# A fused attention and mixture-of-experts layer: the first unit spread by chunks, the last tokens combined by pieces, one small background piece a half step, tails by one queue, VectorE copies in the last unit

## The chip, the cores and the metric

The kernel runs on one core of a Trainium2 chip. The time is the device time of one execution in microseconds (us); "the median" is over several executions. A separate execution was recorded by the hardware profiler, and all rows of the profile are of that one. Engines are written PE (TensorE; PEld are its weight loads), DVE (VectorE), ACT (ScalarE), POOL (GpSimd) and SP (SyncE, which here only issues DMAs). "SPq" and "ACTq" are DMA issues from the queue of SP or ACT.

## What is computed

The input `x` is 8 sequences of 1024 tokens of 256 numbers, all float32. Two stages follow each other, each with a residual:

```
x = x + layernorm(attention(layernorm(x)))     # 16 heads of 16, causal softmax, output matrix Wo
x = x + layernorm(moe(layernorm(x)))           # router over 8 experts, softmax, the best 2 of 8
moe:  gate, up = x @ gate_up[e] + bias         # 256 -> 2 x 512
      act = (clip(up) + 1) * gate * sigmoid(1.702 * gate)
      out = sum over the two experts of weight * (act @ down[e] + bias)
```

## The kernel before, in words

**Attention.** The work is cut into 32 units (`u`): a sequence `b` of 8 and a group `g` of 4 heads. For a unit, q and k of the 4 heads lie in the tiles `qP` and `kP`, each head in 16 rows of its own band of 32 partitions; `spread` (L614) brings them there by eight DMAs from the projected tiles `unq` and `unk`. A unit has nine steps (`STEPS`, L634 to L647), each with two pairs of heads, so 18 half steps. A unit passes through twice: first the maxima of its scores are found (`maxima_tiles`, scores `sa`, L693), then, one unit later, the scores are made again transposed (`values_tiles`, scores `sb`, L788), ACT takes the exponential (L796), and the weighted sums with v are accumulated in `av` (L825). So in the main loop (L1144) a half step holds the `sa` scores of one pair of unit u and the `sb` scores of one pair of unit u-1, the sums of an earlier step, and then pieces of background work. Step 0 of a unit reads only the first 512 columns of `kP` and `qP`.

**Background pieces.** Everything else is written as generators that yield the cost of their next piece on PE, DVE, ACT and POOL: preparing the next sequence (`prep`: layernorm, transposes `xps`), its projections (`project`, `values`), the normalising of the sums (`normalize`, transposes `avt`), the output matrix (`finish`: transposes `aps`, product `yps`) and the routing (`route`: transposes `x2ps`, logits `lpsT`, counts `cps`). Three lists (urgent, due, back) hold the jobs. `earn` (L1079) adds credit for each engine every half step, `affordable` (L1083) finds the first piece that credit allows, `spend` (L1091) emits one, and `pump` (L1102) emits pieces until none is affordable. Pieces of 1.75 us on PE are emitted in place of the sums of the first pair (`whole`, L1203), and in the half steps that hold both kinds of scores `pump` is called with `most=1.0` (L1220), which admits pieces of up to 1.0 us on PE. The tiles in PSUM for `sb` and for all pieces come from one pool of three banks (`ps_b`). Within the attention stage PE, DVE, ACT and SP run in the order of the source (L1131).

**The start.** `begin` (L456) loads and transposes the weights, normalises the 1024 tokens of the first sequence in two chunks of 512, and projects q and k of group 0 chunk by chunk (`project_chunk`, L595; the results are copied by ACT, L602). Half of the normalising steps are ACT's (L488), half DVE's (L486). When both chunks are done, `spread(0)` (L1137) issues q's DMAs from SP and k's from ACT (L622). Then `others` (L525) issues its loads from SP (router weights `rwr`, biases), and its pieces follow: the transposes of Wv and Wo, of `rwr` (L544) and of the biases (L548).

**The experts.** Every token is scattered by POOL (indirect DMAs, L1044) into the regions of its two experts in `xs_dram`. When the last tokens are routed, `fill_tails` (L252) writes 256 rows of zeros behind each expert's last row, eight DMAs, odd experts from ACT's queue and even ones from SP's, each with an address that the issuing engine reads from a table. 71 tiles of 256 rows then pass through gate, up and down (`quarter`, `lower_half`); the rest of the background is pumped in the first ten tiles, and what is left is forced out (`finish_all`, L1460). The loads of tile i+2 are issued from SP at tile i.

**The end.** `both(t)` (L1351) combines 512 tokens: it loads `x1` and the two experts' rows (`yy`, 1 MB, L1358), weighs and adds them in four blocks of 128 tokens (ACT L1372, DVE L1377), takes mean and variance of each block, then one reciprocal root for all four (POOL, L1389), and normalises, adds and writes 512 KB (L1408). The last call stands after the last tile.

Of the kernel before, what the change touches and what calls it, by code (L numbers as in the profile page):

```python
# [17 lines left out]
P = 128  # L18
EPS = 1e-5
# [39 lines left out]
def attn_moe_kernel(  # L59
# [192 lines left out]
    def fill_tails():  # L252

        tail = small.tile([P, E], F32, tag="tail", name="tail")
        nc.vector.tensor_tensor(tail, counts[:, NT, :], region[:, 0, :], ALU.add)
        itail = small.tile([P, E], I32, tag="itail", name="itail")
        nc.vector.tensor_copy(itail, tail)
        for e in range(E):
            queue, engine = (
                (nc.scalar, mybir.EngineType.Activation) if e % 2  # L260
                else (nc.sync, mybir.EngineType.SP)
            )
            at = loaded(itail[0:1, e : e + 1], E * R, engine)
            apart(queue.dma_start(out=slot_rows(at), in_=zeros), "xs")

# [146 lines left out]
    with ExitStack() as attn:  # L412
# [43 lines left out]
        def begin():  # L456
# [54 lines left out]
            for t in range(NC):  # L511
                if t:
                    for kt in range(KT):
                        turn_x(0, t, xn, kt)
                for name in ("q", "k"):
                    project_chunk(0, 0, name, t)
            for mx in mxs:
                in_order(nc.gpsimd.memset(mx, NEG))
            for vp in vps:
# [91 lines left out]
                    yield piece(pe=1.75, act=0.6, after=0 if c else 1)  # L611
                    project_chunk(b, g2, name, c)

        def spread(u):  # L614

            b, g = divmod(u, NG)
            row = qPs[u % NU].rearrange("(h r) (a n s) -> h r a n s", r=HS, n=TN, s=D)
            for a in range(S // (TN * D) if u >= NU else 0):
                nc.sync.dma_start(out=row[:, DH, a], in_=zeros[:HG, :, :D])
            for name, dsts in (("q", qPs), ("k", kPs)):  # L620

                queue = nc.scalar if u == 0 and name == "k" else nc.sync  # L622
                for hh in range(HG):
                    queue.dma_start(
                        out=dsts[u % NU][ds(hh * HS, DH), :],
                        in_=uns[b, g // 2, name][ds((g % 2 * HG + hh) * DH, DH), :],
                    )


# [237 lines left out]
        def finish(b, c):  # L867
# [223 lines left out]
        def spend(least=0.0, most=9.0):  # L1091


            found = affordable(least, most)
            if found:
                kind, job = found
                for i, cost in enumerate(job.cost):
                    credit[i] -= cost
                emit(kind, job)
            return found is not None  # L1100
# [30 lines left out]
        with tc.manual_schedule(  # L1131
# [12 lines left out]
            for u in range(B * NG + 1):  # L1144
# [12 lines left out]
                for k in range(K):  # L1157
# [15 lines left out]
                    for pair in range(2):  # L1173
# [22 lines left out]
                        if first and second:  # L1196
# [3 lines left out]
                            if pair:  # L1200
                                halves = (0, 1) if whole else (1,)
                            else:
                                whole = spend(least=1.5) and bool(late) and (  # L1203
                                    len({t[0] for t in STEPS[late[0][1]][2]}) == 1
                                )
                                halves = () if whole else (0,)
# [141 lines left out]
        yield  # L1348


    def both(t):  # L1351

        x1 = ap2.tile([P, NTB, D], F32, tag="y", name=f"x1_{t}")
        nc.sync.dma_start(out=x1, in_=x1_dram[t])
        yy = x_buffer(f"yy_{t}")[:, : NTB * TOPK * D].rearrange(
            "p (n r d) -> p n r d", n=NTB, r=TOPK
        )
        load = nc.sync.dma_start(  # L1358
            out=yy,
            in_=yt_dram[ds(t * TB * TOPK, TB * TOPK), :].rearrange(  # L1360
                "(p n r) d -> p n r d", p=P, n=NTB
            ),
        )
        ahead_of(load, "yt")
# [3 lines left out]
        mv = small.tile([P, NTB, 2], F32, tag="mv", name="mv")  # L1368

        for n in range(NTB + 1):  # L1370
            if n < NTB:
# [12 lines left out]
        ve = small.tile([P, NTB], F32, tag="ve", name="ve")  # L1384
        nc.vector.tensor_scalar(
            ve, mv[:, :, 1:2].rearrange("p n c -> p (n c)"), EPS, None, ALU.add
        )
        rstd = small.tile([P, NTB], F32, tag="rstd", name="rstd")
        in_order(nc.gpsimd.tensor_tensor(rstd, ve, nhalf, ALU.pow))  # L1389
        yield  # L1390
        yield

        shift = small.tile([P, NTB], F32, tag="shift", name="shift")
        nc.vector.scalar_tensor_tensor(
            shift, mv[:, :, 0:1].rearrange("p n c -> p (n c)"), -1.0, rstd, ALU.mult, ALU.mult
        )
        yield
        o = ap2.tile([P, NTB, D], F32, tag="aT", name=f"o_{t}")
        for n in range(NTB + 1):
            if n < NTB:  # L1400
                nc.scalar.activation(
                    o[:, n, :], acc[:, n, :], AF.Identity,
                    bias=shift[:, n : n + 1], scale=rstd[:, n : n + 1],
                )
            if n:
                nc.vector.tensor_tensor(o[:, n - 1, :], o[:, n - 1, :], x1[:, n - 1, :], ALU.add)
            yield
        nc.sync.dma_start(out=out_t[t], in_=o)  # L1408

    def tiles_for(r):  # L1410

# [5 lines left out]
    with tc.manual_schedule(engines={engines.PE, engines.DVE, engines.Activation}):  # L1417
# [95 lines left out]
```

## Time and profile before

| what | us |
|---|---|
| median of 3 runs | 2243.09 (2241.66 to 2244.4) |
| profiled execution, its own time | 2249.26 |
| its span | 2247.5 |
| start, first scores to the end of unit 0's own part | 31 to 70 |
| units with both kinds of scores | 70 to 1385 |
| the last unit's sums | 1385 to 1420 |
| experts, with background until 1510 | 1420 to 2222 |
| after the last product | 2222 to 2247.5 |
| PE busy over the span | 2178.3 (97%) |
| DVE, ACT, POOL busy | 1641.6, 1092.2, 1063.8 |

How to read the rows: a line of the timeline has the start in us from the span's beginning, the duration, the engine, the line of the source, the operation, the tile written and the tiles read, the shapes, the number of instructions merged into the row, and in brackets the idle time of the engine just before it with what ended it. The ends of matmuls are modelled, so that a matmul that waits may look like a long one. A float32 matmul appears as two instructions.

### The profile page before, as it was taken

To read this page: it belongs to the slowest core of one execution; us is meant where nothing else is said; L and a number is where in the kernel's file an instruction comes from. 1 tells how busy PE (TensorE), PEld (TensorE's weight loads), DVE (VectorE), ACT (ScalarE), POOL (GpSimd) and SP (SyncE) were. 2 spreads that over 40 slices of the span, in tenths; PEclk is the share of its full clock that TensorE was granted. 3 is DMA by queue.
4 is the path that set the end of the run, shared out by engine and by line. 5 is a ranking of instruction groups with operands and counts; after the bars stand their busy time and mean duration, and the time that the engine had idled before them with its cause. 6 is when DMAs were issued, how large, how long until landed. Compare 5 with 4: busy or idle time off the path is not lost.

```text
span 2247.5 us, 45169 instructions
## 1 busy us (share of the span) xinstructions
PE 2178.3 (97%) x16801; PEld 1362.9 (61%) x16801; DVE 1641.6 (73%) x3766; ACT 1092.2 (49%) x2181; POOL 1063.8 (47%) x1228
## 2 busy tenths in 40 slices
PE   7999999999999999999999999989999999999995
PEld 3444444445444445445445444678888888888884
DVE  4766777767767877777777787576568888888775
ACT  3466665665666666666656666522122222322222
POOL 3321463573563472573472463364444444454543
PEclk9899999999999999999999999999999999999998
DMA  3101102101111111211111111676567877877773
GB/s 81 35 6 40 21 21 59 36 24 41 48 30 38 51 30 30 59 30 29 51 39 21 49 49 40 214 218 207 200 227 262 267 264 267 270 245 270 246 250 104
DMA packets 140659, 251.17 MB, mean 112 GB/s; under 512 B 17472, under 2 KB 103384, under 8 KB 138392
## 3 DMA queue, kind: packets, MB, share of 16 engines
q1 hardware_dynamic: 125720, 210.90, 30.3%
q0 software_dynamic: 12960, 35.54, 4.2%
q8 instruction: 133, 2.18, 0.4%
q10 hardware_dynamic: 1760, 1.84, 0.3%
q14 instruction: 86, 0.70, 0.1%
HBM read 175.74 MB, written 55.76 MB: 103 GB/s over the span
## 4 chain that ended last, share of the span: by engine, by line
PE 82%; DVE 10%; POOL 4%; issue 3%; ACT 1%; DMA 1%; POOLq 0%; SPq 0%; ACTq 0%; DVEq 0%
PE sa L693 20%; PE gu L1300 17%; PE av L825 12%; PE dn L1331 8%; PE sb L788 7%; PE vps L584 3%; PE yps L884 3%; PE pjk L598 3%; PE pjq L598 3%; PE avt L856 1%; DVE acc L1377 1%; PE xtps L1280 1%; DVE act L1321 1%; POOL pT L805 1%; DVE gate L1309 1%
## 5 line engine op out<-in xcount | busy, mean ns | idle before, releaser
L796 ACT ACTIVATE pT<-sb 128x512 f32<-128x512 f32 x1152 | 625.5, 595 | 411.7 <-PE sb L788 388.9
L788 PE MATMUL sb<-qP,kP 32*128 32x512 f32 (+3 forms) x3072 | 717.7, 525 | 3.1 <-ACT pT L796 1.1
L693 PE MATMUL sa<-kP,qP 32*128 32x512 f32 (+3 forms) x3072 | 660.3, 528 | 3.6 <-DVE mx L703 1.7
L1300 PE MATMUL gu<-xsT,wg 128*128 128x256 f32 x2272 | 517.5, 380 | 0.7 <-ACT xsT L1282 0.7
L1300 PEld LDWEIGHTS gu<-xsT,wg 128*128 128x128 f32 x2272 | 432.0, 191 | 59.9 <-ACT xsT L1282 0.9
L805 POOL TENSOR_SCALAR_AFFINE_SELECT pT<-pT 128x512 f32<-128x512 f32 x256 | 159.3, 638 | 578.0 <-ACT pT L796 568.4
L709 DVE TENSOR_REDUCE mx<-sa 128x2 f32<-128x1024 f32 x256 | 311.6, 1219 | 118.2 <-PE sb L788 114.5
L1311 ACT ACTIVATE sig<-gate 128x256 f32<-128x256 f32 x284 | 118.3, 416 | 564.7 <-DVE gate L1309 561.8
L693 PEld LDWEIGHTS sa<-kP,qP 32*128 32x128 f32 x3072 | 230.3, 185 | 196.5 <-issue 108.3
L825 PE MATMUL av<-pT,vpad 128*32 128x256 f32 (+1 forms) x5120 | 347.2, 368 | 1.2 <-DVE avs L836 0.9
L1316 POOL TENSOR_TENSOR sig<-sig,gate 128x256 f32<-128x256 f32 x284 | 210.7, 744 | 279.4 <-ACT sig L1311 277.5
L788 PEld LDWEIGHTS sb<-qP,kP 32*128 32x128 f32 x3072 | 305.2, 185 | 39.3 <-ACT pT L796 6.9
L825 PEld LDWEIGHTS av<-pT,vpad 128*32 128x32 f32 x5120 | 116.5, 109 | 288.8 <-issue 216.7
L1331 PE MATMUL dn<-wd,act 128*128 128x256 f32 x1136 | 273.3, 381 | 10.8 <-DVE act L1321 10.4
L1309 DVE TENSOR_SCALAR gate<-gu,bs 128x256 f32<-128x256 f32 x284 | 135.7, 478 | 158.2 <-PE gu L1300 143.4
L1331 PEld LDWEIGHTS dn<-wd,act 128*128 128x128 f32 x1136 | 209.2, 190 | 42.6 <-DVE act L1321 17.7
L703 DVE CUSTOM_DVE_ANT_0 sa<-sa,cmask 128x512 f32<-128x512 f32 x256 | 178.2, 697 | 54.7 <-PE sb L788 32.7
L1341 POOL DMA_INDIRECT ytd<-ys,places x142 | 142.3, 1002 | 137.8 <-DVE ys L1337 111.9
L1044 POOL DMA_INDIRECT xsd<-xn,slots x128 | 126.0, 984 | 61.4 <-issue 31.2
L1321 DVE SCALAR_TENSOR_TENSOR act<-up,sig 128x256 f32<-128x256 f32 x284 | 130.4, 459 | 18.3 <-POOL sig L1316 18.3
L718 DVE TENSOR_REDUCE mx<-sa 128x2 f32<-128x512 f32 x128 | 88.0, 688 | 65.4 <-PE sb L788 38.2
L1313 DVE TENSOR_SCALAR up<-gu,bs 128x256 f32<-128x256 f32 x284 | 134.5, 474 | 0.0
(202 smaller groups left out, 2394.8 us busy)
## 6 DMA issues: line engine op xcount, KB each, us to landing
wg<-_L_ffn_gate_up_proj_dram SPq DMA_DIRECT2D x71, 1024.0 KB
wd<-in_L_ffn_down_proj_dram SPq DMA_DIRECT2D x71, 512.0 KB
xs<-xsd SPq DMA_DIRECT2D x67, 258.0 KB
yy<-ytd SPq DMA_DIRECT2D x16, 1024.0 KB
bs<-biasd SPq DMA_DIRECT2D x71, 132.0 KB
x<-in_L_attn_x_dram SPq DMA_DIRECT2D x16, 512.0 KB
qP<-unq SPq DMA_DIRECT2D x128, 64.0 KB
x1d<-y SPq DMA_DIRECT2D x16, 512.0 KB
```

The source lines that it names most:

```text
L693: nc.tensor.matmul(ps[:, hh, ds(at, w)], lhsT=qP[r, ts(i, P)], rhs=kP[r, ds(c * QC, w)], start=True, stop=True,)
L703: nc.vector.tensor_tensor_reduce(out=ps[:, hh, :], in0=ps[:, hh, :], in1=cmask, scale=1.0, scalar=NEG, op0=ALU.add, op1=ALU.max, accum_out ...
L709: nc.vector.tensor_reduce(mx[:, heads, i, 2:3], ps, AX.X, ALU.max)
L788: nc.tensor.matmul(banks[hh][:, ds(at, QC - off)], lhsT=kP[r, ts(j, P)], rhs=qP[r, ds(c * QC + off, QC - off)], start=True, stop=True,)
L796: nc.scalar.activation(pT[:, 2 * pair + hh, :], banks[hh], AF.Exp)
L805: in_order(nc.gpsimd.affine_select(out=d, in_=d, compare_op=ALU.is_ge, fill=0.0, base=0, pattern=[[0, HG], [1, P]], channel_multiplier=-1,))
L825: nc.tensor.matmul(av[ds(hh * HS, HS), ds(off + a - at, z - a)], lhsT=vp[:, j, ds((g * HG + hh) * VS, HS)], rhs=pT[:, hh, a:z],  start=c n ...
L1300: nc.tensor.matmul(ps[:, half, :], lhsT=wg[:, kt, ds(half * FF + f * P, P)], rhs=xT[:, kt, :], start=(kt == 0), stop=(kt == KT - 1),)
L1309: nc.vector.tensor_scalar(gt, ps[:, 0, :], bs[:, f : f + 1], LIMIT, ALU.add, ALU.min)
L1316: in_order(nc.gpsimd.tensor_tensor(sg, sg, gt, ALU.mult))
L1321: nc.vector.scalar_tensor_tensor(act[:, f, :], up, 1.0 - LIMIT, sg, ALU.max, ALU.mult)
L1331: nc.tensor.matmul(ps[:, n, :], lhsT=act[:, f, ts(n, P)], rhs=wd[:, f, :], start=(f == 0), stop=(f == FT - 1),)
```

## The change

It has five parts.

1. *Start.* `spread` takes a range of columns. `begin` calls it after each chunk of 512, so that there are 16 DMAs of half the length in place of 8, all from SP's queue; the call after `begin` is gone. In the second chunk ACT does all four normalising steps.
2. *Pump.* `spend` returns the cost of the piece that it emitted. In the half steps where `most` is 1.0 or less, `pump` admits only pieces below 0.3 us on PE once it has emitted one of 0.3 or more.
3. *Tails.* All eight zero fills are issued from SP's queue, and SP reads the eight addresses.
4. *Last unit.* In `finish` of the first chunk of the last sequence, the copies of `aT` and `y` out of PSUM are DVE's (`tensor_copy`) in place of ACT's.
5. *End.* The last call of `both` loads `yy` by four DMAs, one a block, and takes the reciprocal root, the shift, the normalising and the output write in two halves of two blocks. For other calls the order of the work is as before.

```
-            at = loaded(itail[0:1, e : e + 1], E * R, engine)
-            apart(queue.dma_start(out=slot_rows(at), in_=zeros), "xs")
+            at = loaded(itail[0:1, e : e + 1], E * R)
+            apart(nc.sync.dma_start(out=slot_rows(at), in_=zeros), "xs")
...
-                    if n % 2:
+                    if n % 2 and t == 0:
                         ln_apply(xn[:, n, :], of, mv, rstd, n)
...
                 for name in ("q", "k"):
                     project_chunk(0, 0, name, t)
+                spread(0, ts(t, QC))
...
-        def spread(u):
+        def spread(u, cols=slice(0, S)):
...
-                queue = nc.scalar if u == 0 and name == "k" else nc.sync
                 for hh in range(HG):
-                    queue.dma_start(
-                        out=dsts[u % NU][ds(hh * HS, DH), :],
-                        in_=uns[b, g // 2, name][ds((g % 2 * HG + hh) * DH, DH), :],
+                    nc.sync.dma_start(
+                        out=dsts[u % NU][ds(hh * HS, DH), cols],
+                        in_=uns[b, g // 2, name][ds((g % 2 * HG + hh) * DH, DH), cols],
                     )
...
-                nc.scalar.copy(aT[:, kt, :], ps.rearrange("p n q -> p (n q)"))
+                copy = nc.vector.tensor_copy if last and c == 0 else nc.scalar.copy
+                copy(aT[:, kt, :], ps.rearrange("p n q -> p (n q)"))
...
-                nc.scalar.copy(y[:, ts(n2, 2), :], ps)
+                copy(y[:, ts(n2, 2), :], ps)
...
-            while spend(most=most):
-                pass
+            while True:
+                got = spend(most=most)
+                if not got:
+                    break
+                if got[0] >= 0.3 and most <= 1.0:
+                    most = min(most, 0.29)
...
-            spread(0)
...
-    def both(t):
+    def both(t, final=False):
...
+        if final:
+            for n in range(NTB):
+                nc.sync.dma_start(out=yy[:, n], in_=of[:, n])
+        else:
+            ahead_of(nc.sync.dma_start(out=yy, in_=of), "yt")
...
+        size = NTB // 2 if final else NTB
...
+            if n and n % size == 0:
+                g = slice(n - size, n)
+                nc.vector.tensor_scalar(
+                    ve[:, g], mv[:, g, 1:2].rearrange("p n c -> p (n c)"), EPS, None, ALU.add
+                )
+                in_order(nc.gpsimd.tensor_tensor(rstd[:, g], ve[:, g], nhalf[:, g], ALU.pow))
...
+        for g in (slice(a, a + size) for a in range(0, NTB, size)):
+            nc.vector.scalar_tensor_tensor(
+                shift[:, g], mv[:, g, 0:1].rearrange("p n c -> p (n c)"), -1.0, rstd[:, g],
+                ALU.mult, ALU.mult,
+            )
             yield
+            for n in range(g.start, g.stop + 1):
...
+            nc.sync.dma_start(out=out_t[t][:, g], in_=o[:, g])
...
-            ends.append((0, both(routed[r])))
+            ends.append((0, both(routed[r], r == NT - 1)))
```

More of the change, by code (lines that the diff above doesn't have):

```diff
@@ L258, in fill_tails @@
         for e in range(E):
[L259 to L262, printed above, removed]
-            at = loaded(itail[0:1, e : e + 1], E * R, engine)
-            apart(queue.dma_start(out=slot_rows(at), in_=zeros), "xs")
+            at = loaded(itail[0:1, e : e + 1], E * R)
+            apart(nc.sync.dma_start(out=slot_rows(at), in_=zeros), "xs")
     LATE = 4
@@ L1096, in spend @@
                 kind, job = found
+                found = job.cost
                 for i, cost in enumerate(job.cost):
@@ L1099, in spend @@
                 emit(kind, job)
-            return found is not None
+            return found
         def pump(*us, most=9.0):
@@ L1202, in attn_moe_kernel @@
                             else:
-                                whole = spend(least=1.5) and bool(late) and (
+                                whole = spend(least=1.5) is not None and bool(late) and (
                                     len({t[0] for t in STEPS[late[0][1]][2]}) == 1
@@ L1357, in both @@
         )
[L1358 to L1362, printed above, removed]
-        )
-        ahead_of(load, "yt")
+        of = yt_dram[ds(t * TB * TOPK, TB * TOPK), :].rearrange(
+            "(p n r) d -> p n r d", p=P, n=NTB
+        )
+        if final:
[3 more added lines that the diff above has]
+            ahead_of(nc.sync.dma_start(out=yy, in_=of), "yt")
         yield
@@ L1368, in both @@
         mv = small.tile([P, NTB, 2], F32, tag="mv", name="mv")
+        ve = small.tile([P, NTB], F32, tag="ve", name="ve")
+        rstd = small.tile([P, NTB], F32, tag="rstd", name="rstd")
+        shift = small.tile([P, NTB], F32, tag="shift", name="shift")
+        size = NTB // 2 if final else NTB
         for n in range(NTB + 1):
@@ L1383, in both @@
             yield
[L1384 to L1389, printed above, removed]
+            if n and n % size == 0:
[4 more added lines that the diff above has]
+                in_order(nc.gpsimd.tensor_tensor(rstd[:, g], ve[:, g], nhalf[:, g], ALU.pow))
         yield
         yield
[L1393 to L1397, printed above, removed]
-        o = ap2.tile([P, NTB, D], F32, tag="aT", name=f"o_{t}")
[L1399 to L1406, printed above, removed]
-            yield
-        nc.sync.dma_start(out=out_t[t], in_=o)
+        o = ap2.tile([P, NTB, D], F32, tag="aT", name=f"o_{t}")
+        for g in (slice(a, a + size) for a in range(0, NTB, size)):
[3 more added lines that the diff above has]
+            )
+            yield
+            for n in range(g.start, g.stop + 1):
+                if n < g.stop:
+                    nc.scalar.activation(
+                        o[:, n, :], acc[:, n, :], AF.Identity,
+                        bias=shift[:, n : n + 1], scale=rstd[:, n : n + 1],
+                    )
+                if n > g.start:
+                    nc.vector.tensor_tensor(
+                        o[:, n - 1, :], o[:, n - 1, :], x1[:, n - 1, :], ALU.add
+                    )
+                yield
+            nc.sync.dma_start(out=out_t[t][:, g], in_=o[:, g])
     def tiles_for(r):
```

## The prediction

> **What bounds it.** I read the page first: the PE row, the granted clock and the chain's shares.
>
> ```profile
> PE   7999999999999999999999999989999999999995
> PEclk9899999999999999999999999999999999999998
> PE 82%; DVE 10%; POOL 4%; issue 3%; ACT 1%; DMA 1%; POOLq 0%; SPq 0%; ACTq 0%; DVEq 0%
> ```
>
> TensorE is the bound nearly everywhere, and the change alters none of its arithmetic. So it can win only where TensorE stands still or streams late: in the first slices, inside "busy" half steps, and in the last slice. The timelines of those places come next.
>
> **First unit.** Timeline and windows (us, busy of PE, PEld, DVE, ACT, POOL, then granted clock):
>
> ```profile
> 13.21 8.07 DVE L399 TENSOR_SCALAR xn<-x,mv,rstd 128x256 f32<-128x256 f32 x2
> 21.03 1.65 PE L443 MATMUL xps<-ident,xn 128*128 128x128 f32 x7 [3.56 <-DVE xn L399]
> 27.97 2.52 ACTq L624 DMA_DIRECT2D kP<-unk  x4
> 28.89 0.54 SPq L528 DMA_DIRECT2D rwr<-L_ffn_router_weight_dram  x1
> 30.97 0.44 PE L450 MATMUL wps_o<-ident,wr_o 128*128 128x128 f32 x2 [2.54 <-ACT wvT L451]
> 33.94 2.08 PE L693 MATMUL sa<-kP,qP 32*128 32x512 f32 x4
> 20.00:24.00 4.00, 2.97 (x9) 1.97 (x10) 1.29 (x2) 1.17 (x2) 0.82 (x1) 0.67 0.00 0
> ```
>
> VectorE's two normalising steps take 8.07 us beside GpSimd's memsets (the same form took 0.41 at 9.79), and TensorE waits 3.56. The clock is then 0.67 in that window. Later ACT issues four DMAs before it can empty the weights' transposes: TensorE waits 2.54.
>
> With the change ACT does all four steps. Two took 1.09 from 13.51, so four end near 15.7, before the transposes reach them at 17.2; VectorE's removed steps cost nothing elsewhere. At full speed the second chunk repeats the first: from its first transposes (taken as 1.0, the row of eight at full clock later) to the end of the `unk` copy about 5.5 us, so 22.7 and not 27.9. The 3.56 and about 1.5 of half clock go. But all 16 spreading DMAs (before 8) are now on SP, 0.63 us each (2.53 for four). q of chunk 0 starts at 16.3, k ends at 21.3; chunk 1 runs 21.3 to 26.4. Queued behind are `rwr` (0.54) and `gubr` (0.53), ending near 27.5, and the biases. A 64 KB DMA landed at most 2.2 us after issue (a wait for `kP` ended at 30.80, issue 28.57), so `gubr` is there at 29.7. The first pair of scores needs only chunk 0 and runs near 24; the two small transposes L544 and L548 stand behind it in TensorE's order and wait for those loads; the second pair follows at about 30.0. Before: 33.94. **Gain 3.9.** If each score waited for both chunks (last landing 28.6), the mark would be 31 to 32, a gain of 2; with the loads in time, 7.5. I take 3.9, since the issue rows give it.
>
> The new hole from 25 to 29 costs clock too; before, the rows had half clock after the holes, and I leave that as it is. [...]
>
> **Half steps.** A half step is a pair's maxima scores `sa` and weights' scores `sb`, then weighted sums `av` and background pieces. Two small pieces in one look like this (PE, then ACT):
>
> ```profile
> 495.49 1.09 PE L942 MATMUL x2ps<-ident,xn 128*128 128x128 f32 x8
> 496.51 0.48 PE L693 MATMUL sa<-kP,qP 32*128 32x256 f32 x2
> ...
> 497.33 0.79 PE L788 MATMUL sb<-qP,kP 32*128 32x256 f32 x3
> 498.04 0.64 PE L825 MATMUL av<-pT,vpad 128*32 128x256 f32 x8
> 496.32 1.11 ACT L943 COPY xT<-x2ps 128x512 f32<-128x512 f32 x2
> ```
>
> `av` starts 1.53 after `sa`, where the good steps show 1.07 (495.49 is 0.57 after an `av` at 494.92): 0.46 lost inside "busy" TensorE, since `sb` needs a bank that ACT empties only at 497.4. The planner's costs, followed through the source, put two pieces of 0.3 or more into one half step 28 times. I cut TensorE's rows from 70 to 1385 into 554 half steps and subtracted 1.07 for scores, 0.57 for one `av` (1.0 for several), 0.59, 0.5 or 1.91 for a piece. What is left, in the step itself and in the next: no piece 0.14 and 0.10; one 0.25 and 0.07; two 0.2 and 0.34 (19 cases); two and a transposed maximum 0.21 and 0.53 (9); one and a maximum 0.19 and 0.39. Splitting a double: 0.54 plus an empty step's 0.24 becomes twice 0.32, a gain of 0.14; with a maximum 0.98 becomes 0.90. So 19 x 0.14 + 9 x 0.08 = **3.4**. Upper end: all of the following lateness goes, 19 x 0.34 + 9 x 0.53 = 11.2. Lower: each moved piece brings a lone piece's 0.32 and removes nothing but 0.2, minus 28 x 0.12 = -3.4. I take 3.4, the measured difference of like rows. The pieces go one or two half steps later; forced emission does not set in, as the last q/k projection is done at least 14 half steps ahead of its deadline in every batch.
>
> **Tails.** SP gets four more zero fills, ACT loses four.
>
> ```profile
> 1494.77 4.40 ACTq L264 DMA_DIRECT2D xsd<-zeros  x4
> 1498.42 0.43 DVE L1321 SCALAR_TENSOR_TENSOR act<-up,sig 128x256 f32<-128x256 f32 x1 [3.99 <-POOL sig L1316]
> 1498.90 0.82 PE L1331 MATMUL dn<-wd,act 128*128 128x256 f32 x2 [4.08 <-DVE act L1321]
> 1500.14 0.42 ACT L1311 ACTIVATE sig<-gate 128x256 f32<-128x256 f32 x1 [6.27 <-DVE gate L1309]
> ```
>
> ACT's next step waits for a gate that VectorE makes from 1499.57, and VectorE and TensorE (4.08) wait for GpSimd, whose product stands behind scatters. So freeing ACT is worth **0**. On SP, four took 7.66 including a 3.3 wait for an earlier fill; eight end by 1505 to 1510, ahead of the load of `xs` at 1508.93. That load then waits for the fills to land (5.6 before) and may go at 1512 to 1516; its user, the transposes at 1527.2, covers it (18 us). Bounds: +2 if ACT's release lets something earlier run, -1 if weights come late.
>
> **Last unit's copies.** The `aT` copies (ACT 1.11 for two at 1409.84) and two of `y` (0.58 each) go to VectorE, idle for 13.76 us there; its 128x512 copy out of PSUM takes 0.69. The scores at 1410.13 took 1.52 for 1.14: **0.3**, at most 1, and a loss of 0.2 if the longer copy comes last.
>
> **End.**
>
> ```profile
> 2229.18 0.32 SPq L1358 DMA_DIRECT2D yy<-ytd  x1
> 2234.06 1.70 ACT L1372 ACTIVATE acc<-yy,chosen_w 128x256 f32<-128x256 f32 x4 [12.84 <-DMA yy<-ytd]
> 2238.94 0.17 DVE L1385 TENSOR_SCALAR ve<-mv 128x4 f32<-128x4 f32 x1
> 2243.03 0.39 SPq L1408 DMA_DIRECT2D out_dram<-o  x1
> ```
>
> 1 MB lands 4.56 after its issue. A quarter lies between the small DMA's 2.2 and 4.56; linear in bytes 2.8, so 2232.3, and the others 0.4 to 0.6 apart, faster than VectorE's 1.04 per block. VectorE's chain ends near 2237.2 (one more `ve`, 0.2), then GpSimd's 1.04 for the second half, while ACT and VectorE do the first half: its add ends at 2239.2, then shift 0.2, two activations and the last add, 1.8: 2241.0. **Gain 2.0**, and 0.2 for half as much to write last: 2.2. The ends: 4, if the first piece lands at once; -1, if pieces land as late as the whole. [...]
>
> **Sum.** 3.9 + 3.4 + 0 + 0.3 + 2.2 = 9.8. The profiled execution took 2249.26 (span 2247.5, 1.76 around it), so 2239.5 by its own time. The median of the runs shown is 6.17 lower (2243.09), which gives 2233.3.
>
> **Rivals.**
> - The half steps return nothing, the rest does: 6.4, so 2236.7; with the end worth nothing either, 2238.9. For it: the 0.14 per double is small beside its scatter. It is also the case in which one part doesn't do what it says.
> - All lateness after doubles goes: 11.2 in place of 3.4, 2225.5. For it: the bank wait seen at 497.33 is entirely a double's. Against it: half steps with one piece lose 0.25 as well.
> - Slower: routing of the last tokens slips past the deadline at tile 10, where all that is left is forced out. Place: 1493 to 1509. Price: eight scatters 1.27 apart, 10.2, the table's chain (1504.2 to 1509.1) 4.9, and two half-clock windows of 3.4, so 3.4 more: 18.5, less 9.8, +8.7: 2251.8. It decides once pieces slip a whole tile, some 12 pump calls. Against it: the limit does not hold in the last unit's sums or the experts, and 28 pieces are spread over 31 units.
>
> **Chances.** Forecast 0.60, within 2229 to 2238.6; all lateness gone 0.14; half steps nothing 0.20 (0.11 of it still faster); late routing 0.06. A measurement here can tell 0.2%, 4.5 us, from no change. So faster 0.85, same 0.10, slower 0.05. The range 2224 to 2241 takes in both first rivals and the low ends.
>
> **What would show it.** No VectorE wait at the second chunk's transposes, L544 waiting for `rwr` instead, the second pair of scores near 30; no two small pieces in a half step between two score groups, and fewer `av` over 1.2 after `sa`; the 4.08 at the tails still there, behind GpSimd; the first `acc` near 2.8 after the first `yy`, the last output write 2 us nearer to it. I am wrong if the spread's end sets the scores, if moved pieces bring the same lateness to their new place, or if a stretch I left alone (half clock at 65 to 79) grows.

## The result and the profile after

The median went from 2243.2 us to 2242.67 (22 runs each); the ratio is 1.0, with a 95% interval of 0.999 to 1.0009. The forecast was 2233.3 with a range of 2224 to 2241: no change can be told from these runs, and the time lies outside the range.

The profiled executions alone would tell another story: 2249.26 before and 2242.13 after, 7.1 apart. But before's lies 6.1 above its own median and after's 0.5 below. Before's has half clock at 1144 (6.8 us) and at 1393 (3.4 us), which the trace of the change does not have (clock 1.00 from 1140 to 1150 and from 1380 to 1400); the stretches that hold them account for 3.6 and 1.6 of the difference. So from here on single traces are used for places, and many timed runs for sizes of the whole.

The page of the changed kernel has the same shape (rows of the page, in 40 slices, and the chain's shares):

```profile
PE   7999999999999999999999999989999999999995
PEclk8899999999999999999999999999999999999998
PE 83%; DVE 8%; POOL 4%; issue 2%; ACT 1%; DMA 1%; SPq 1%; ACTq 0%; DVEq 0%; POOLq 0%
```

The second digit of PEclk fell from 9 to 8: that is the first unit.

**First unit.** Timeline of the changed kernel:

```profile
13.44 2.08 ACT L485 ACTIVATE xn<-x,shift,rstd 128x256 f32<-128x256 f32 x4
16.34 1.04 PE L439 MATMUL xps<-ident,xn 128*128 128x128 f32 x8
23.75 2.43 SPq L620 DMA_DIRECT2D kP<-unk  x4
26.22 0.53 SPq L526 DMA_DIRECT2D rwr<-L_ffn_router_weight_dram  x1
28.04 0.35 PE L542 MATMUL rps<-ident,rwr 8*128 8x8 f32 x2 [4.21 <-DMA rwr<-L_ffn_router_weight_dram]
29.13 2.07 PE L689 MATMUL sa<-kP,qP 32*128 32x512 f32 x4
```

VectorE's 8.07 and TensorE's wait of 3.56 at the second chunk's transposes are gone, and the second pair of scores comes at 29.13 in place of 33.94, near the 30.0 of the prediction. In front of it TensorE now waits 4.21 for `rwr`. What that wait brings stands in the windows (busy PE, PEld, DVE, ACT, POOL, then granted clock), of the changed kernel first, then of before:

```profile
24.00:28.00 4.00, 0.00 (x0) 0.00 (x0) 1.52 (x4) 0.00 (x0) 0.00 (x0) 0.80 0.18 43
28.00:32.00 4.00, 3.48 (x9) 1.74 (x10) 1.30 (x5) 0.00 (x0) 0.00 (x0) 0.50 0.07 11
32.00:36.00 4.00, 4.00 (x13) 2.68 (x14) 0.80 (x3) 0.59 (x1) 0.00 (x0) 0.50 0.83 176
36.00:40.00 4.00, 4.00 (x11) 2.52 (x8) 0.69 (x1) 0.59 (x1) 0.00 (x0) 0.50 0.54 74
```

```profile
28.00:32.00 4.00, 1.46 (x6) 1.04 (x8) 0.00 (x0) 1.29 (x4) 0.00 (x0) 0.95 0.69 128
32.00:36.00 4.00, 4.00 (x12) 1.31 (x9) 1.86 (x7) 0.00 (x0) 0.00 (x0) 0.50 0.05 3
36.00:40.00 4.00, 4.00 (x18) 2.80 (x16) 1.51 (x4) 0.59 (x1) 0.00 (x0) 0.69 0.97 193
```

TensorE is "busy" from 28 to 40, but at half clock throughout, in one piece of 13.65 us that began at 26.4, in the wait; before, the piece after the hole was 6.8. The lead over before shrinks from 4.81 at the second pair to 1.75 at the first transposed scores (69.96, now 68.21). Both are leads over this one execution of before; others started sooner, as the experiments show.

**Half steps.** Where before had two transposes `x2ps` in one half step (495.49, eight matmuls), the changed kernel has four in one and four in another:

```profile
487.35 0.66 PE L940 MATMUL x2ps<-ident,xn 128*128 128x128 f32 x4
487.94 0.38 PE L689 MATMUL sa<-kP,qP 32*128 32x128 f32 x2
...
497.06 0.66 PE L940 MATMUL x2ps<-ident,xn 128*128 128x128 f32 x4
497.64 0.70 PE L689 MATMUL sa<-kP,qP 32*128 32x512 f32 x2
```

The rule does what it says, but the two pieces now lie 9.71 us apart. With half steps of 2.4 us on average (1315 us over 554 of them) that is about four, where the prediction had one or two. And units 4 to 23, free of half clock in both traces, took 859.5 before and 859.6 after.

**Tails.** SP issues all eight, and the wait behind GpSimd is still there (2.75; 4.08 before):

```profile
1490.89 0.42 DVE L1324 SCALAR_TENSOR_TENSOR act<-up,sig 128x256 f32<-128x256 f32 x1 [3.97 <-POOL sig L1319]
1491.37 1.22 PE L1334 MATMUL dn<-wd,act 128*128 128x256 f32 x2 [2.75 <-DVE act L1324]
1492.10 8.19 SPq L260 DMA_DIRECT2D xsd<-zeros  x8
```

But the whole stretch from the first gate of the experts to tile 9 (I call it the routing stretch) took 123.2 in place of 119.3.

**End.** From the end of the last product to the end of the span 21.49, before 24.09:

```profile
2224.62 1.75 SPq L1367 DMA_DIRECT2D yy<-ytd  x4
2228.56 2.43 ACT L1381 ACTIVATE acc<-yy,chosen_w 128x256 f32<-128x256 f32 x4 [11.87 <-DMA yy<-ytd]
2231.37 0.17 DVE L1395 TENSOR_SCALAR ve<-mv 128x2 f32<-128x2 f32 x1
2233.71 0.17 DVE L1395 TENSOR_SCALAR ve<-mv 128x2 f32<-128x2 f32 x1
2235.55 2.04 SPq L1420 DMA_DIRECT2D out_dram<-o  x2
```

So three places are left to explain: what the hole costs, where the half steps' gain went, and why the routing stretch grew.

### The profile page after: what moved, and what is told of

It reads as the page before. It is cut to its first block, busy times and chain, and to the rows that moved or that the text cites. A ratio compares the mean times of both kernels' runs of the same rounds, so it can differ in the third digit from the quotient of the medians.

```text
span 2240.4 us, 45184 instructions
## 1 busy us (share of the span) xinstructions
PE 2172.7 (97%) x16801; PEld 1356.0 (61%) x16801; DVE 1646.1 (73%) x3770; ACT 1090.1 (49%) x2179; POOL 1065.0 (48%) x1229
## 4 chain that ended last, share of the span: by engine, by line
PE 83%; DVE 8%; POOL 4%; issue 2%; ACT 1%; DMA 1%; SPq 1%; ACTq 0%; DVEq 0%; POOLq 0%
PE sa L689 20%; PE gu L1303 18%; PE av L821 12%; PE dn L1334 9%; PE sb L784 7%; PE vps L582 3%; PE yps L882 3%; PE pjk L596 3%; PE pjq L596 2%; PE avt L852 1%; PE xtps L1283 1%; DVE acc L1386 1%; POOL pT L801 1%; DVE gate L1312 1%; PE aps L872 1%
## 5 line engine op out<-in xcount | busy, mean ns | idle before, releaser
L784 PEld LDWEIGHTS sb<-qP,kP 32*128 32x128 f32 x3072 | 298.8, 184 | 40.0 <-ACT pT L792 7.5
```

Source lines behind the costliest of these rows:

```text
L784: nc.tensor.matmul(banks[hh][:, ds(at, QC - off)], lhsT=kP[r, ts(j, P)], rhs=qP[r, ds(c * QC + off, QC - off)], start=True, stop=True,)
```

## The experiments

Each timed run has a span and a mean granted clock of TensorE. I split the mean span of a kernel's runs in two: span x (1 - clock), the *clock loss*, and what remains, the *rest* (work and waits). Not all of the loss costs time: in the traces 15.7 to 21.8 us of half clock, so 8 to 11 of each loss, stand behind the last product, where TensorE has no more to do. Only differences of the loss count, and a shorter end lowers it too. Ratios are to runs of before on the same chip, taken together with the kernel's; the loss and the rest of before were 26.1 to 27.1 and 2215.3 to 2216.0 over the four such groups.

| kernel | median | ratio (95%) | clock loss | rest |
|---|---|---|---|---|
| the change | 2242.67 | 1.0 (0.999 to 1.0009) | 28.3 | 2213.1 |
| e1 start alone | 2240.68 | 0.9987 (0.9976 to 0.9997) | 25.0 | 2213.7 |
| e2 pump alone | 2247.16 | 1.0023 (1.0011 to 1.0035) | 31.5 | 2215.1 |
| e3 tails alone | 2243.92 | 0.9997 (0.9984 to 1.0009) | 26.2 | 2215.3 |
| e4 end alone | 2240.63 | 0.9989 (0.9978 to 0.9999) | 25.7 | 2213.4 |
| e5 pump, units 0 to 29 | 2243.75 | 1.0003 (0.9992 to 1.0014) | 26.5 | 2215.6 |
| e6 pump, from unit 28 | 2250.05 | 1.0033 (1.0022 to 1.0044) | 30.7 | 2217.1 |
| e7 change + early loads | 2233.91 | 0.9961 (0.9949 to 0.9973) | 21.8 | 2210.4 |
| e8 e7 + pump to unit 29 | 2230.38 | 0.9945 (0.9929 to 0.996) | 20.8 | 2207.5 |
| e9 change + late pieces | 2235.45 | 0.9965 (0.9954 to 0.9976) | 25.7 | 2208.4 |
| e10 e7 + pump to unit 7 | 2227.81 | 0.9932 (0.9915 to 0.9949) | 20.0 | 2206.1 |
| e11 two calls left out | 2250.67 | 1.003 (1.0017 to 1.0042) | 28.5 | 2220.2 |
| e12 one call left out | 2244.55 | 1.0003 (0.9989 to 1.0016) | 26.9 | 2215.4 |
| e13 change + slack | 2238.18 | 0.997 (0.9959 to 0.9982) | 22.9 | 2214.3 |
| e14 e10 + slack | 2230.72 | 0.9944 (0.9931 to 0.9958) | 20.4 | 2209.6 |
| e15 early loads alone | 2244.07 | 0.9998 (0.9988 to 1.0008) | 26.0 | 2216.0 |

### Four parts, each alone (e1 to e4)

Each is before with one part's lines of the diff shown above.

> Before, with part 1 of the change alone (the first unit spread by chunks, all sixteen DMAs from SP, ACT taking all four normalising steps of the second chunk). My theory now: the start's gain is mostly taken back by half clock after the new hole at 24 to 28, so the first scores come 8 to 9 earlier, the second pair 4 to 5 earlier, but the first transposed scores of unit 0 (69.96 before) only 1 to 2.5 earlier, and the whole is 1 to 2.5 faster (about 0.999). The prediction's own sizing: 3.9 faster at 70 and at the end (0.9983). Rival: half clock takes all of it, 0 (1.000).

> Before, with part 2 alone (after a piece of 0.3 us or more, only smaller ones in the same half step). My theory now: units 2 to 24, where neither trace has half clock, gained only about 0.7, so the doubles' own lateness was nearly all that a lone piece costs too; the time is 0 to 1.5 faster (0.9993 to 1.000). The prediction's sizing: 3.4 faster (0.9985). Rival: the stretch of the last tokens' routing, which took 3.9 longer with the whole change, is later because pieces slip; then the stretch from the first gate to tile 9 (119.3 before) is 2 or more longer here, and the whole 0 to 3 slower.

> Before, with part 3 alone (all eight zero fills from SP's queue). Theory A: the 3.9 that the routing stretch (first gate to tile 9, 119.3 before) lost with the whole change come from here, because SP's loads of weights and tiles stand behind eight fills: 2 to 4 slower (1.001 to 1.002) and that stretch at 121 to 123. Theory B: the prediction's 0, the stretch within 1.5 of before, but for a window of half clock more or less; the 3.9 come from where the half-clock windows fall.

> Before, with part 5 alone (the last tokens' rows loaded by four DMAs, statistics and output in two halves). Both the prediction and the theory: from the end of the last product to the end 21.5 in place of 24.09, nothing else moved, 2.2 to 2.6 faster (0.9989). Rival: the four loads compete with nothing and the gain is there, but the time is the same within 1, since the end of the span is not what the device time counts.

The start alone is 2.9 us faster (0.0013 of 2243.7), the end 2.5, the tails within 0.7 of nothing. The start stands a little above my 1 to 2.5 and below the prediction's 3.9, but its interval (0.7 to 5.4) holds both. Part 2 alone is slower by 5.2 by the ratio (3.4 by the medians), beyond all that I had written down, and nearly all of it is clock loss (31.5 against 26.4). Its trace is 2.7 ahead of before at unit 24 (2.1 of it from unit 1, where before has twice as much half clock) and 1.0 behind at tile 9: the routing stretch took 126.6. The four add up to -0.9. That agrees with the change, but each of them is known to some 2.5 only.

The traces of these and the later runs also show how much the start of before varies. Nine traces start as before does (before, e2 to e6, e11, e12, e15). In six of them VectorE's two normalising steps take about 8 us, and the second pair of scores comes at 33.2 to 33.9. In e4, e12 and e15 they take 4.3 to 5.2, and the second pair comes at 27.8 to 28.7, no later than with the new start and its hole (28.6 to 29.1 in the change, e1 and e13). Rows of e12:

```profile
12.87 4.33 DVE L399 TENSOR_SCALAR xn<-x,mv,rstd 128x256 f32<-128x256 f32 x2
25.61 0.50 PE L450 MATMUL wps_o<-ident,wr_o 128*128 128x128 f32 x2 [2.54 <-ACT wvT L451]
28.71 2.08 PE L693 MATMUL sa<-kP,qP 32*128 32x512 f32 x4
```

The first transposed scores come at 64.3 to 70.2 in the nine, 68.5 in the mean, and at 67.6 to 68.2 in the three. So the prediction took the start's price from an execution with the long wait. Why the wait varies is not known.

### Which pieces of the rule cost (e5, e6)

```
-                if got[0] >= 0.3 and most <= 1.0:
+                if got[0] >= 0.3 and most <= 1.0 and u < 30:     # e5
+                if got[0] >= 0.3 and most <= 1.0 and u >= 28:    # e6
```

The planner is deterministic, so its choices can be listed from the source: with e5 every piece from the last unit's sums on is that of before, with e6 every one is that of part 2 alone.

> Before, with part 2 alone, but its rule applies only in units 0 to 29; from unit 30 on the pieces are chosen as before, so the last tokens' routing pieces come in the calls of before (last piece in call 654, not 657). Theory: what part 2 cost (1.0023) is the later routing pieces of the last tokens among the first experts. Then the attention units keep the gain of 2 to 4 that the run with part 2 alone had at units 8 to 24, the stretch from the first gate to tile 9 is back near 119 (126.6 with part 2 alone), and the whole is 1.5 to 4 faster than before (0.9982 to 0.9993). Rival: moved pieces bring their lateness to the new place all along, and the gain at units 8 to 24 was chance; then 1.001 to 1.0025 again.

> Before, with part 2 alone, and its rule only from unit 28 on, so all pieces up to there are those of before, and those of the routing among the first experts are those of part 2 alone (last piece in call 657). Theory: the stretch from the first gate to tile 9 takes 123 to 127 in place of 119.3, no other stretch changes by more than a window of half clock, and the whole is 4 to 8 slower (1.002 to 1.0035). Rival: within 1 of before (1.0005 or less).

e6 is 6.2 slower by the medians (7.4 by the ratio) although nothing differs up to unit 28: the cost is the last units' shift alone. Its largest waits of TensorE from 1400 to 1545 us, which take in the routing stretch (engine, line and tile that waited, for whom: us in total, times, longest):

```profile
PE cps L1003 <- DVE chosen L999: 3.3, 2, 3.1
PE firstps L323 <- DVE seg L320: 3.0, 1, 3.0
PE x2ps L942 <- ACT xn L919: 2.2, 4, 1.7
PE tabps L347 <- DVE two L344: 2.1, 1, 2.1
PE dn L1337 <- DVE act L1327: 1.6, 2, 1.2
```

Before's there:

```profile
PE dn L1331 <- DVE act L1321: 5.8, 2, 4.1
PE cps L1003 <- DVE chosen L999: 2.8, 2, 1.7
```

The rule carries over 2 to 3 planner calls into the experts. `firstps`, `x2ps` and `tabps` now meet a producer that isn't done. Half clock follows three of the gaps (of 1.69, 3.10 and 2.99, ended at 1443.5, 1476.4 and 1502.7): 13.6 us in this trace (from 1446, 1477 and 1504), 6.8 before.

e5 takes that cost away, but shows no gain either (my 1.5 to 4 is missed), so the first theory's other half fell: the half steps return next to nothing. The traces say why. Medians of the time of four units, in us, over eight traces without the rule (before, e1, e3, e4, e6, e11, e12, e15) and seven with it (the change, e2, e5, e7, e8, e9, e13), leaving out those with half clock in these units:

| units | without | with |
|---|---|---|
| 4 to 7 | 170.3 | 168.8 |
| 8 to 11 | 173.0 | 172.6 |
| 12 to 15 | 171.4 | 172.6 |
| 16 to 19 | 173.0 | 172.6 |
| 20 to 23 | 171.6 | 172.6 |
| 24 to 27 | 173.0 | 172.6 |

Over units 2 to 29 the sum is -0.9: -1.5 in units 4 to 7, +2.3 in 12 to 15 and 20 to 23, and -1.7 in the rest. The three batches that stand out are those in which a large piece changes its unit. In 12 to 15 and 20 to 23, before ran eight `pjk` matmuls in the third unit of the batch and none in its last (as the traces of before and of the change show); with the rule four of them, and sixteen `x2ps` in place of eight, fall into the last, as they do in other batches of before. In 4 to 7 it is the other way round: before had four and four, and the rule puts all eight into the third unit. So what splitting doubles is worth shows in the rest, where no `pjk` crosses: -1.7 over 14 units. Whether that is the forecast's 0.14 per double is not shown, since the doubles in these units were not counted. That the crossing `pjk` makes the rest of the difference is argued from its place in each batch; no run moved it alone.

### The hole (e7, e9, e15)

e7 issues two loads at the start, behind those of Wq and Wk; e15 does only that, on before. e9 leaves the loads and moves the pieces.

```
+            rwr = wr["r"] = ap2.tile([E, D], F32, tag="xT", name="rwr")
+            nc.sync.dma_start(out=rwr, in_=router_w)          # e7, e15: in begin
...
             jobs["p1"] = start(due, project(0, 1))
+            due.remove(more)                                  # e9
+            due.append(more)
```

> The whole change, with the loads of the router weights and the gate's biases issued at the start, behind those of Wq and Wk, where SP is idle from 3.4 to 16. Theory: the hole at 23.8 to 28.0 goes, the second pair of scores runs at 24 to 25.5 in place of 29.1, the half clock of 27 to 41 is gone or down to one window, and the first transposed scores come at 62 to 65.5 in place of 68.2: 3 to 6 faster than the whole change (0.9974 to 0.9987 of before). Rival 1: VectorE's maxima, which TensorE waits for from 50 on, set the pace there; the first transposed scores come at 66.5 or later, and 0 to 2 are gained (0.9992 to 1.000). Rival 2: the hole moves to the scores that wait for the second chunk, at 28 to 30, and brings the same half clock: 0 to 1.5.

> The whole change, with the loads where it has them, but the two small pieces that wait for them (transposes of the router weights and of the gate's biases, L542 and L546) put behind the values and the second projection of the first sequence, so that TensorE has other work from 23.8 to 28. Theory: the hole and the half clock after it were the cost, however the hole is filled: second pair of scores at 24 to 25.5, no half clock until 45, first transposed scores at 57 to 59.5 in place of 68.2, and 0.9949 to 0.9975 of before, within 1.5 us of the run with the early loads. Rival: what the early loads gained lies in the freer queue of SP (the later spreads, the biases): then 0.998 or more.

> Before, with nothing but the early loads of the router weights and the gate's biases. Theory: before, nothing waits for them long, since the spread's end is what the second pair of scores waits for (its 33.94 moves by less than 1); the whole is 0 to 1 faster (0.9996 to 1.0003). So the early loads are worth their 9 only where the spread by chunks has made the hole. Rival: they are worth as much without the spread by chunks, 4 or more (0.998 or less).

Timeline of e7:

```profile
23.50 1.13 PE L690 MATMUL sa<-kP,qP 32*128 32x512 f32 x4
24.46 0.23 PE L543 MATMUL rps<-ident,rwr 8*128 8x8 f32 x2
24.62 0.27 PE L547 MATMUL gubps<-ident,gubr 64*128 64x64 f32 x1
24.82 1.13 PE L690 MATMUL sa<-kP,qP 32*128 32x512 f32 x4
25.88 1.99 PE L583 MATMUL vps<-wvT,xnT 128*128 128x256 f32 x8
```

No hole, and the clock is 1.00 in every window from 20 to 44: `vps` takes 1.99 where it took 3.78 after the hole. The first transposed scores come at 58.07 in place of 68.21, 10.1 earlier: about 4.2 of wait and half of 13.65. The whole is 8.8 faster than the changed kernel (2242.67 to 2233.91; more than my 3 to 6). e9 fills the hole with other work and gains 7.2, with those scores at 56.03: the hole is the cause, not the queue. The time is 1.54 above e7's (run on another chip); from those scores to unit 2 its trace has 18.3 us of half clock, e7's 11.5. e15 is worth nothing (0.9998). In its trace the second pair does come 6.16 earlier than in before's, at 27.78, against what I expected; but e4 and e12 have it at 28.54 and 28.71 without the early loads, with VectorE's short steps.

How much half clock a hole brings is less fixed. The three traces with the hole of 4.2 have 13.65 (the change, e1, e13), and the five without any hole there none before 53 us (e7 to e10, e14). Of the nine that start as before does, eight have 6.8 at this place and e12 has 13.65, behind no longer wait than 2.54.

### Both edits, and less of the rule (e8, e10)

> The whole change with both edits: early loads, and the rule of part 2 only in units 0 to 29. Theory: start 5 to 8, half steps 2 to 3.5, end 2.5, tails 0, together 9 to 13 faster than before (0.9942 to 0.9960), faster than either kernel. Rivals: without the start's part (VectorE sets it) 5 to 7 (0.9970 to 0.9978); without the half steps' 7 to 10.

> The best version so far (the whole change, early loads, rule of part 2 only in units 0 to 29), with the rule only in units 0 to 7; the pieces from unit 8 on are then those of before. Theory: the rule gains 1.7 in units 4 to 7, then 0.4 in a batch of four units, but loses 1.2 in units 12 to 15 and 20 to 23, where the fourth projection of k moves from the third unit of the batch into the last. So here units 4 to 7 take 168.4 to 168.8 (before 170.4), units 12 to 15 take 171.3 to 171.5 (172.6 with the rule), where no half clock falls in; the whole is 0 to 1 faster than the best (0.9935 to 0.9960 of before). Rival: the 1.2 were chance of those runs, and units 12 to 15 take 172.6 again.

e8 is 3.5 faster than e7 on the same chip, and they differ only in the rule from unit 30 on; their intervals overlap a little. It is 13.5 faster than before by the medians, just beyond my estimate, and within it by the ratio (0.9945). e10 takes the rule away from unit 8 on: units 4 to 7 took 168.8, units 12 to 15 171.4 as without the rule, as expected, and at 2227.81 it is the fastest kernel here, faster than both kernels of this case; its interval overlaps e8's.

### What decides the routing stretch (e11 to e14)

```
-                if i + AHEAD < EARLY:
+                if i + AHEAD < EARLY and (i or f > 1):    # e11
+                if i + AHEAD < EARLY and (i or f):        # e12
```

e13 and e14 put one call more between a producer and the TensorE piece that reads it, for the last tokens only:

```
-                yield piece(pe=0.5, act=0.6, after=0 if kt else 2)
+                yield piece(pe=0.5, act=0.6, after=0 if kt else 2 + more)
-            yield piece(pe=0.6, dve=0.2, after=1 + more)
+            yield piece(pe=0.6, dve=0.2, after=1 + 2 * more)
-        yield piece(pe=0.3, dve=0.9, after=2)
+        yield piece(pe=0.3, dve=0.9, after=3 if nr == NT else 2)
-        yield piece(pe=0.5, dve=0.6, after=2)
+        yield piece(pe=0.5, dve=0.6, after=3 if nr == NT else 2)
```

> Before, with the first two of four planner calls in the first expert tile left out, so that the last tokens' routing comes one call (a quarter of a tile) later in the same order (last piece in call 655). Theory A: what counts is how the two chunks' pieces interleave, since that sets the gaps; here both are still routed side by side (second logits in call 621), the stretch from the first gate to tile 9 takes 118.5 to 121.5, and the whole is 0 to 2 slower (1.000 to 1.001). Theory B: each call of lateness costs the same, as 3 calls cost 6.2: 2 slower (1.0009), with the stretch at 121 to 122.5.

> Before, with only the first planner call of the first expert tile left out. The last piece comes in call 661, seven calls late, and the second chunk's logits eleven calls late (631), behind the first chunk's counts, as under the rule. Theory A (the interleaving sets the gaps): the stretch from the first gate to tile 9 takes 122 to 127 as in all four runs with the chunks routed one behind the other, 3 to 7 slower (1.0013 to 1.0032). Theory B (each call costs 2): 14 slower (1.006), the stretch at 133.

> The whole change, with one planner call more between a piece of the last tokens' routing and the TensorE piece that reads it (transposes x2ps, counts cps, the table's firstps and tabps); the last piece comes in call 661 in place of 657. Theory: the stretch from the first gate to tile 9 takes about 106 us of work, plus TensorE's waits (12.1 with the whole change), plus half of the time at half clock (10.2); later pieces find their input ready, so the waits fall to 7 to 10 and the half clock to 0 to 6.8, the stretch to 113 to 119 from 123.2, and the whole is 3 to 7 faster than with the change (0.9968 to 0.9988 of before). Rival: the length of the chain decides, and four calls more make the stretch 123 or longer (1.000 or slower).

> The best version so far (the whole change, early loads, the rule only in units 0 to 7) with the same slack in the last tokens' routing. Theory: waits of TensorE in the stretch 6 to 9 (10.3 in the order of before), half clock 0 to 6.8, the stretch 112 to 118 in place of 119, and 1 to 5 faster than without the slack (0.991 to 0.9928 of before). Rival: in this order the waits are behind GpSimd's scatters (4.08 and 1.7), which no slack of the routing's pieces removes: within 1.5 of the version without (0.9928 to 0.9942).

Both theories of e11 and e12 fell: one call late lost 6.7 (1.003), seven calls late 0.7 (1.0003). The traces, with TensorE's gaps between matmul rows summed over the stretch:

| kernel | stretch | gaps | half clock | stretch - gaps - half clock / 2 |
|---|---|---|---|---|
| before | 119.3 | 10.3 | 6.8 | 105.6 |
| the change | 123.2 | 12.1 | 10.2 | 106.0 |
| e2 | 126.6 | 11.5 | 20.4 | 104.9 |
| e6 | 125.0 | 12.9 | 13.6 | 105.3 |
| e10 | 116.8 | 8.8 | 3.4 | 106.3 |
| e11 | 124.7 | 13.4 | 10.2 | 106.2 |
| e12 | 119.5 | 9.2 | 6.8 | 106.9 |
| e13 | 122.3 | 12.2 | 6.8 | 106.7 |
| e14 | 122.9 | 14.1 | 6.8 | 105.4 |

The last column, what the work would take without gaps at full clock, is the same within 2.0, while the stretches differ by 9.8: the cost is the gaps and half the half clock, and no lengthening of the work. The order of the pieces changes where the gaps fall. How was not to be foreseen from the planner: the slack brought e13 the time expected (0.997), but not for my reason, since the gaps stayed at 12.2 and only the clock loss fell (22.9 against 28.3); in e14 it cost 2.9, though the interval overlaps e10's. There the waits (same columns as above) grew:

```profile
PE dn L1335 <- DVE act L1325: 5.7, 2, 3.9
PE cps L1002 <- DVE chosen L998: 3.3, 2, 2.4
PE lpsT L948 <- ACT xT L942: 2.5, 1, 2.5
PE tabps L343 <- DVE two L340: 1.9, 1, 1.9
```

e10's, without the slack:

```profile
PE dn L1335 <- DVE act L1325: 3.7, 2, 2.0
PE cps L1002 <- DVE chosen L998: 2.8, 2, 1.9
PE lpsT L948 <- ACT xT L942: 0.8, 1, 0.8
```

What stays open is which order gives small gaps, and why one gap is followed by more half clock than another. A kernel without GpSimd's scatters ahead of its product was not tried.

## Why the prediction was wrong

Most of what was missed lies in part 2: it was forecast 3.4 faster and is 5.2 slower alone (e2), 8.6 of the 9.3 between the forecast's 9.8 and the medians' 0.5.

- **Start, 3.9: the order of events right, the clock left out, the baseline a long case.** The second pair came at 29.13 for the forecast 30.0. The step that failed is "The new hole from 25 to 29 costs clock too; before, the rows had half clock after the holes, and I leave that as it is": the piece of half clock after the hole is 13.65, in before's trace 6.8, and of the lead of 4.81 only 1.75 was left at the first transposed scores. Timed alone, the part gave 2.9 (0.7 to 5.4), which does not exclude 3.9. That it comes so near is partly luck: the 8.07 of VectorE, on which the price rests, is the long case of two. Filling the hole gains another 8.8 (e7), three times what the part brings with it.
- **The clock after the hole.** The piece of half clock lasts from 26.4 to 40.1. TensorE's rows are full by the profile's modelled ends (4.00 of 4.00 from 32 to 36 and from 36 to 40), and the clock stays at 0.50 in both windows: 8 us of rows without a pause did not end it.
- **Half steps, 3.4: the term that failed.** The step is "The pieces go one or two half steps later", free of charge. In the change two pieces of one double ended four half steps apart; large pieces crossed into other units, which, by their place in the batches, cost 2.3 in two of them and gained in one; and the shift was carried into the last units and the experts, which the sum put at nothing. Units 2 to 29 gained 0.9 in the traces and nothing in time (e5, 1.0003), and the last units' shift alone costs 6.2 (e6). The size of 0.14 per double is not shown by itself. The first rival, which had the half steps return nothing, was right on them, but kept all other gains.
- **The routing of the last tokens: the slower rival's place, given 0.06.** It named the stretch (1493 to 1509) and more half clock there (10.2, before 6.8; a piece of 3.4, the length of its windows, is in before's trace at 1393), though the longest wait of the change, 3.09, ends at 1475, ahead of it. Its price of 18.5 was not right (the stretch grew by 3.9), and its deadline at tile 10 never came into it: the last routing product of the change, `tabps`, runs at 1505, tile 10 begins at 1549. "Against it: the limit does not hold in the last unit's sums or the experts" is true and beside the point: credits and order are carried over, and a shift of 2 to 3 calls costs 5 to 7 (e2, e6). That is not a price per call: one call late cost 6.7 (e11), seven calls late nothing clear (e12).
- **Tails, 0:** right within what the runs can tell (0.9997, 0.9984 to 1.0009).
- **Last unit's copies, 0.3:** right. From the first scores of the last unit's sums to TensorE's first gate product 36.2 to 36.3 with them (e8, e10, e14) and 36.6 without (e3, e5, e11, e12), each without half clock. The rows of the changed kernel:

```profile
L886 DVE COPY y<-yps 128x512 f32<-128x512 f32 x2 | 1.4, 692 | 6.6 <-PE yps L882 6.6
L875 DVE COPY aT<-aps 128x512 f32<-128x512 f32 x2 | 1.4, 691 | 1.2 <-PE aps L872 1.1
```

- **End, 2.2:** right, 2.6 in the trace and 2.5 timed (0.2 to 4.9). Its parts were not: the first quarter came 3.9 after its issue, not 2.8, and the four activations end 6.4 after it.

Sum by the timed parts: -2.9 + 5.2 - 0.7 - 2.5 and the copies' 0.3 make -1.2, against the -9.8 of the forecast and the -0.5 of the medians. Of the 9 missed, an estimate from these parts gives some 5 to 6 to the routing, 2 to 3 to the half steps and 1 to the start; each part's interval is 2 to 3 wide to either side.

## What to carry to other kernels

Price a new hole of the bound engine with the clock after it, and take the longest piece of half clock that the trace shows (here 13.65, which before has at 65.7 behind a wait of 1.20); a load of 0.5 us, issued late, cost 9. Price a wait that is to go from more than one execution: VectorE's 8.07 was 4.3 to 5.2 in a third of them. Where a planner hands out work by credits, an edit in one stage moves the order in the next: list its choices there before and after, and look at the pieces that wait for a serial chain. And compare single profiles by stretches without half clock only, since one execution carries several us of chance (before's 2249.26 is 6.1 above its median).

## What the runs showed of the hardware

- Half clock came in pieces of 3.4 (before, at 1393), 6.8 (before, at 1144), 13.65 (the change, at 26.4) and once 20.5 us (e9, from 53.9), also while TensorE's rows had no pause (4.00 of 4.00 from 32 to 40 in the change). In the first unit a hole of 4.2 came with 13.65 in all three traces that have it (the change, e1, e13), a wait of 2.54 with 6.8 in before and with 13.65 in e12; a gap of 1.7 (e6, at 1442) was followed by a piece of 3.4, where one of the same length (before, at 1441) had none after it (1.00 to 1456).
- Executions of one kernel differ by 10 us and more (2237.25 to 2249.17 for before in 35 runs), and in the 22 runs of the changed kernel the span went with the mean granted clock: the longest, 2247.2, at 0.985 and the shortest, 2237.6, at 0.990 (correlation -0.85).
- VectorE's two normalising steps of the second chunk took 8.07 in one trace (before, beside GpSimd's memsets from 13.05 to 20.82) and 4.33 in another of the same code (e12); ACT took 2.08 for four (the change).
- Eight DMA issues with an address read from a table took 8.19 on SP's queue alone (the change), and before with all eight there took no longer within what the runs tell (e3, ratio 0.9997, 0.9984 to 1.0009).
